# Picking and comparing neighbour marks for two graphs at once in a graph network on one core

One core of a Trainium2 chip; the metric is the time of one execution on the device in microseconds (us).

## The reference, cut to what matters

128 graphs of 64 nodes with 128 features, and a 0/1 adjacency matrix each (a seventh to an eighth of it ones). For every pair (i, j) of nodes a message is computed by a three-layer MLP, masked by the adjacency, summed over j, and the sums update the nodes by a second MLP.

```python
pair_feats = jnp.concatenate([f_i, f_j], axis=-1)
messages = _mlp(pair_feats, ...)                 # relu, layernorm, relu, layernorm, linear
messages = messages * coupling_matrix[..., None]
agg = jnp.sum(messages, axis=2)
updated = part_feats + _mlp(concatenate([part_feats, agg]), ...)
```

## The kernel before

It computes messages only where the adjacency has a one. Each graph gets 640 edge slots; two graphs make a pair (64 pairs), 512 slots a chunk (160 chunks), so five chunks serve two pairs. For a pair a 0/1 matrix `tp` says which node owns each slot. A selection on TensorE (`marks`) gives for each slot and each of 64 possible neighbours the position at which that neighbour stands; comparing with the slot's number (`compare`, VectorE) leaves a 0/1 mark at the right one. Node and neighbour marks together, 128 rows, gather the first layer's rows for each edge (`layer0`). The steps of all stages are put into a plan by chunk and place, and each engine executes its instructions in that order.

```python
        def marks(n):                                   # chunk n
            MK[n] = ps_k.tile([P, CH * P], F32, name="mk")
            for g, e, c, w in pieces(n):                # one graph at a time
                nc.tensor.matmul(MK[n][:, c:c + w], lhsT=qsall[..., g % 2, :],  # identity | positions
                                 rhs=TP[g // 2][:, e:e + w], start=True, stop=True)
        def compare(n):
            nc.vector.tensor_tensor(S[n], MK.pop(n), cmpt[:, o:o + CH * P], op=ALU.is_equal)
        def layer0(n):
            ...   # hps = abl/abh.T @ s, then h = relu(hps + b0) on ScalarE
        def root_of(q):                                 # once for five chunks
            sd = root0(stp, V0[q], QT, "m20")           # ScalarE, from GpSimd's variances
            nc.scalar.copy(SH[q][:, 0:2, :], sdb)
            nc.gpsimd.tensor_tensor(SH[q][:, 2:4, :], sdb, SH[q][:, 0:2, :]..., op=ALU.subtract)  # sh
        def turn_root(q):
            nc.tensor.transpose(SD[q][...], SH.pop(q)..., ident)                # TensorE needs sh
        ...
            # block b of four pairs starts at chunk o; all three steps run on GpSimd
            at(o - 8, "e", place, b)        # before, mid, pos
            at(o - 7, "e", place_out, b)    # pos * adjacency into the selecting weights
            at(o - 7, "e", odd_marks, b)    # two products over the adjacency
            ...
            # var0_of, root_of and turn_root of group q: chunks n and n + 1, n = 5q + 5
```

Of the kernel before, what the change touches and what calls it, by code (L numbers as in the profile page):

```python
# [9 lines left out]
F32 = mybir.dt.float32  # L10
F16 = mybir.dt.float16
F32R = mybir.dt.float32r
# [11 lines left out]
def tile_gnn(  # L24
# [9 lines left out]
    uw2: bass.AP, ub2: bass.AP,  # L34
    out: bass.AP,
):



# [65 lines left out]
    def load_first(b, q0, q1):  # L105
# [44 lines left out]
    ident = const.tile([P, P], F32, name="ident")  # L150
    make_identity(nc, ident)

    cmpt = const.tile([P, 4 * CAP], F16, name="cmpt")
    nc.gpsimd.iota(cmpt[N:P, :], pattern=[[0, 4], [1, CAP]], base=1, channel_multiplier=0,
                   allow_small_or_imprecise_dtypes=True)
    nc.vector.memset(cmpt[0:N, 0:3 * CAP // 2], 1.0)

    slot = const.tile([P, CAP], F16, name="slot")
    nc.gpsimd.iota(slot, pattern=[[2, CAP]], base=1, channel_multiplier=0,
                   allow_small_or_imprecise_dtypes=True)  # L160

    qsall = const.tile([P, 2, PB, 2, P], F16, name="qsall")
    for k in range(2):
        nc.vector.memset(qsall[:, k], 0.0)
        nc.gpsimd.tensor_copy(qsall[:, k, :, :, 0:N], ident.rearrange("p (g m) -> p g m", g=2)
                              .unsqueeze(1).to_broadcast([P, PB, 2, N]))
    ones_row = const.tile([1, P], F32, name="ones_row")

    cumall = const.tile([P, NP], F32, name="cumall")
# [120 lines left out]
    def edge_path(es):  # L290
        blkp = es.enter_context(tc.tile_pool(name="blk", bufs=3))
        adp = es.enter_context(tc.tile_pool(name="adp", bufs=2))
        tpp = es.enter_context(tc.tile_pool(name="tpp", bufs=10))
        sp = es.enter_context(tc.tile_pool(name="sp", bufs=4))
        hp = es.enter_context(tc.tile_pool(name="hp", bufs=10))
        yp = es.enter_context(tc.tile_pool(name="yp", bufs=13))
        lp = es.enter_context(tc.tile_pool(name="lp", bufs=3))
        wp = es.enter_context(tc.tile_pool(name="wp", bufs=2))
        updp = es.enter_context(tc.tile_pool(name="upd", bufs=1))
# [31 lines left out]
                fn(*args)  # L331

        blocks = {b: {} for b in range(NB)}
        TP, S, H, ST0, V0, SD, SH, Y, ST1, Q, OH, WT, YS, MK, D = ({} for _ in range(15))


        def load_adj(b):
# [7 lines left out]
        def load_x(b):  # L345
            if b < 2:
                blocks[b]["xn"] = xn0[:, b]
                return
            xn = blkp.tile([P, PB, C], F32, name="xn", bufs=7)
            nc.sync.dma_start(xn, xf[b * PB * P:(b + 1) * PB * P, :]  # L350
                              .rearrange("(q p) c -> p q c", p=P))
            blocks[b]["xn"] = xn
# [37 lines left out]
        def place_out(b):  # L390
            blk = blocks[b]
            pos = blk.pop("pos")
            for g in range(2):
                s = slice(g * N, (g + 1) * N)
                nc.gpsimd.tensor_tensor(qsall[s, b % 2, :, g, N:P], pos[s], blk["an"][s],
                                        op=ALU.mult)

        def place_first():
# [7 lines left out]
        def place_pair(q):  # L406
            blk = blocks[0]
            for g in range(2):
                s = slice(g * N, (g + 1) * N)
                nc.vector.scalar_tensor_tensor(qsall[s, 0, q, g, N:P], blk["rk"][s, q],  # L410
                                               blk["before"][s, q:q + 1], blk["an"][s, q],
                                               op0=ALU.add, op1=ALU.mult)

# [19 lines left out]
        def turn_x_out(b, q0=0, q1=PB):  # L433
            blk = blocks[b]
            if q0 == 0:
                blk["xnT"] = blkp.tile([P, PB * P], F32, name="xnT", bufs=5)
            nc.scalar.copy(blk["xnT"][:, q0 * P:q1 * P], blk.pop("x_ps")[:, q0 * P:q1 * P])

        def rows(b, half):
# [10 lines left out]

        def rows_hi(b, half):

            hi = blkp.tile([P, 4, C], F32R, name="abh", bufs=3)
            nc.scalar.copy(hi, blocks[b]["ab_ps", half].rearrange("p (k c) -> p k c", k=4))  # L454
            blocks[b]["hi", half] = hi

        def rows_lo(b, half):
            blk = blocks[b]
            hi = blk.pop(("hi", half))
            lo = blkp.tile([P, 4, C], F32R, name="abl", bufs=3)  # L460
            nc.vector.tensor_tensor(  # L461
                lo, blk.pop(("ab_ps", half)).rearrange("p (k c) -> p k c", k=4), hi.bitcast(F32),
                op=ALU.subtract)
            blk["ab", half] = (lo, hi)


        def distance(p):
            b, q = divmod(p, PB)
            D[p] = tpp.tile([P, CAP], F16, name="d", bufs=3)
            nc.scalar.activation(D[p], slot, AF.Abs, bias=blocks[b]["mid"][:, q:q + 1], scale=-1.0)  # L470

        def make_tp(p):
# [4 lines left out]
                                    op0=ALU.is_lt)  # L477
            TP[p] = tp

        def pieces(n):  # L480

            at_, end = n * CH * P, (n + 1) * CH * P
            while at_ < end:
                g, e = divmod(at_, CAP)
                w = min(end - at_, CAP - e)
                yield g, e, at_ - n * CH * P, w
                at_ += w

        def marks(n):

            MK[n] = ps_k.tile([P, CH * P], F32, name="mk")
            for g, e, c, w in pieces(n):
                nc.tensor.matmul(MK[n][:, c:c + w],  # L493
                                 lhsT=qsall[:, g // (2 * PB) % 2, g // 2 % PB, g % 2, :],
                                 rhs=TP[g // 2][:, e:e + w], start=True, stop=True)

        def compare(n):
            S[n] = sp.tile([P, CH * P], F32R, name="s")
            o = n % QC * CH * P
            nc.vector.tensor_tensor(S[n], MK.pop(n), cmpt[:, o:o + CH * P], op=ALU.is_equal)  # L500

        def layer0(n):

            ps = ps_h.tile([P, CH * P], F32, name="hps")
            s = S.pop(n)
            for g, e, c, w in pieces(n):
                for k, ab in enumerate(blocks[g // (2 * PB)]["ab", g // 4 % 2]):
                    nc.tensor.matmul(ps[:, c:c + w], lhsT=ab[:, g % 4, :], rhs=s[:, c:c + w],  # L508
                                     start=(k == 0), stop=(k == 1))
            H[n] = hp.tile([P, CH * P], F32, name="h")  # L510
            nc.scalar.activation(H[n], ps, AF.Relu, bias=b0c)  # L511
# [143 lines left out]
        def wide(name, u):  # L655

            if name not in u.blk:
                u.blk[name] = updp.tile([P, PB, C], F32, name=name,
                                        bufs=2 if name == "uo" else 1)
            return u.blk[name][:, u.q, :]  # L660

        def sums_out(u):
# [87 lines left out]
        for b in range(NB):  # L750
            o = b * CPB
            if b > 1:
                at(max(o - 25, 0), "a", load_adj, b)
                at(max(o - 20, 0), "a", load_x, b)
            if b > 0:
                r = max(o - 13, 1)
                at(max(o - 14, 0), "m", rank, b)
                at(r, "x", count, b)
                at(r + 1, "a", count_out, b)
                at(r + 1, "a", degrees, b)  # L760
                at(o - 8, "e", place, b)
                at(o - 7, "e", place_out, b)
                at(o - 7, "e", odd_marks, b)
                at(o - 4, "m", odd_weights, b)
                at(o - 3, "x", turn_x, b)
                at(o - 2, "a", turn_x_out, b)
# [34 lines left out]
                at(n + t[14], "m", finish, u)  # L801
        for p in range(NP):
            n = p * TG * 2 // CH
            if n >= 4:
                at(n - 5 if n >= 5 else 0, "a", distance, p)
                at(n - 4, "m", make_tp, p)
            w = p // 2 * QC + QC + L1 + p % 2
            last = p // 2 == NQ - 1
            at(w - 4, "a", node_marks, p)
            at(NCHK + L1 + 1 if last else w + 2, "e1", weights, p)  # L810
            at(NCHK + L1 + 2 if last else p // 2 * QC + SC, "x1", reduce, p)
# [19 lines left out]
        rank(0)  # L831
        count(0)
        count_out(0)
        nc.gpsimd.memset(cmpt[0:N, 3 * CAP // 2:4 * CAP], 1.0)
        turn_x(0, 0, 2)
        turn_x_out(0, 0, 2)
        degrees(0)
# [3 lines left out]
        make_tp(0)  # L841
        rows(0, 0)
        rows_hi(0, 0)
        distance(1)
        place_pair(1)
        make_tp(1)
        marks(0)
        rows_lo(0, 0)
        compare(0)
        nc.vector.memset(ones_row, 1.0)  # L850
        marks(1)
        compare(1)
        at(0, "x", turn_x, 0, 2, PB)
        at(0, "m", lambda: (place_pair(2), place_pair(3)))
        at(1, "a", lambda: turn_x_out_rest())
        at(1, "e", odd_marks, 0)
        at(12, "m", odd_weights, 0)
# [48 lines left out]
        for n in range(last + 1):  # L906
            run(n, "a")
            run(n, "m")
            if 0 <= n - L1 < NCHK:
                layer1(n - L1)  # L910
            run(n, "b")
            if n < NCHK:
                layer0(n)
            if 0 <= n - 1 < NCHK:
                stats0(n - 1)
            if n + 2 < NCHK:
                marks(n + 2)
                compare(n + 2)
            if 0 <= n - L1 < NCHK:
                stats1(n - L1)  # L920
            for k in ("x", "x1", "x2", "e1", "e"):
                run(n, k)
# [166 lines left out]
```

## Time and profile before

| | before |
|---|---|
| time, median of the first 3 runs | 626.22 us (625.81 to 626.4) |
| TensorE, VectorE, ScalarE, GpSimd busy | 95, 80, 56, 58% |
| a block of ten chunks in the steady stage | 35.83 us |
| granted TensorE clock, mean (1 is full speed) | 0.981 |

The profile's main lines are in the prediction below. Two lines also belong here. They are groups of the kernel before (line, engine, operation, names, shapes, count, then busy us and mean ns, then idle us before them and what ended it):

```profile
L541 PE MATMUL ma<-ident,sh 128*80 128x128 f32 x32 | 9.3, 292 | 6.8 <-POOL sh L536 5.6
L541 PEld LDWEIGHTS ma<-ident,sh 128*80 128x80 f32 x32 | 3.8, 119 | 10.5 <-POOL sh L536 10.5
```

The first line is the transpose that turns `sh`, the second the weight load (PEld) just before it; the two idle times are of one wait and are not to be added. Ten microseconds look like nothing in 625. But they say that TensorE's turn of `sh` already waits for GpSimd; in the list of waits the second line counts 18 of 32 times. A chain through a half idle engine had no slack.

### The profile page before, as it was taken

What the parts mean: (1) busy time and instruction counts of PE and PEld (TensorE: products, weight loads), DVE (VectorE), ACT (ScalarE), POOL (GpSimd) and SP (SyncE); (2) the same over time, 40 slices, a digit from 0 to 9 for tenths busy, and PEclk for the clock granted to TensorE, in tenths of its full rate; (3) what the DMA queues carried; (4) which work ended last, traced back from release to release, by engine and by line L of the source; (5) the groups of instructions that cost most, each with busy time, mean ns of one, the idle gap of its engine ahead of it and who ended that gap; (6) DMA issues with size and microseconds to landing.
All of it is one profiled execution on the core that took longest, in us unless ns stands there. A gap on an engine that the chain in (4) does not pass through costs nothing. (4 is left out here: it accounts for less than half of the span.)

```text
span 625.1 us, 15119 instructions
## 1 busy us (share of the span) xinstructions
PE 595.2 (95%) x5521; PEld 545.6 (87%) x5521; DVE 497.8 (80%) x1900; ACT 348.2 (56%) x716; POOL 363.3 (58%) x922
## 2 busy tenths in 40 slices
PE   6899999999999999999999999999999999998875
PEld 5687889999999999999999999999999999997763
DVE  7768778898878788888878789887878888885574
ACT  4565465656656565665656556665656566553412
POOL 5815264855648384664738376574838566452742
PEclk7899999999999999999999999999999999998987
DMA  4401011113030213103022211203030110201001
GB/s 120 67 2 29 12 30 39 30 34 55 1 75 12 56 32 54 33 1 86 1 60 29 56 31 28 58 3 67 21 56 22 39 24 2 60 2 40 23 18 37
DMA packets 70922, 22.52 MB, mean 36 GB/s; under 512 B 53430, under 2 KB 70844, under 8 KB 70844
## 3 DMA queue, kind: packets, MB, share of 16 engines
q1 hardware_dynamic: 70556, 21.38, 15.8%
q8 instruction: 45, 0.74, 0.5%
q14 instruction: 33, 0.27, 0.1%
q10 hardware_dynamic: 288, 0.13, 0.1%
HBM read 6.82 MB, written 4.19 MB: 18 GB/s over the span
## 5 line engine op out<-in xcount | busy, mean ns | idle before, releaser
L521 DVE BATCH_NORM_STATS2 st<-hT 128x6 f32<-128x128 f32 x640 | 140.1, 281 | 58.9 <-PE hT L517 58.5
L557 PEld LDWEIGHTS z<-w1c,h 128*128 128x128 f32 x1280 | 169.2, 192 | 7.2
L557 PE MATMUL z<-w1c,h 128*128 128x128 f32 x1280 | 169.6, 275 | 0.0
L560 ACT ACTIVATE y<-z 128x512 f32<-128x512 f32 x160 | 96.1, 601 | 107.8 <-PE z L557 107.8
L623 POOL TENSOR_TENSOR w<-oh,m_q 128x320 f32<-128x320 f16 x124 | 87.0, 723 | 115.6 <-PE mk L493 100.6
L567 DVE BATCH_NORM_STATS2 st<-y 128x6 f32<-128x128 f32 x640 | 138.0, 278 | 4.9 <-ACT y L560 4.9
L511 ACT ACTIVATE h<-hps,b0c 128x512 f32<-128x512 f32 x160 | 109.3, 683 | 5.8 <-PE hps L508 5.7
L500 DVE TENSOR_TENSOR s<-mk,cmpt 128x512 fp32r<-128x512 f32 x160 | 107.8, 674 | 0.7 <-PE mk L493 0.6
L517 PE MATMUL hT<-ident,h 128*128 128x128 f32 x640 | 97.4, 275 | 0.0
L508 PE MATMUL hps<-s,abl 128*128 128x512 f32 (+3 forms) x256 | 92.4, 373 | 0.0
L517 PEld LDWEIGHTS hT<-ident,h 128*128 128x128 f32 x640 | 76.4, 141 | 9.7
L554 PE MATMUL z<-b1t,sdT 80*128 80x512 f32 x160 | 80.5, 503 | 1.4 <-ACT y L560 1.4
L508 PE MATMUL hps<-s,abh 128*128 128x512 f32 (+3 forms) x256 | 78.8, 326 | 0.0
L638 PEld LDWEIGHTS ys<-y,w 128*64 128x64 f32 x1280 | 69.4, 137 | 9.5 <-issue 9.3
L638 PE MATMUL ys<-y,w 128*64 128x128 f32 x1280 | 77.2, 276 | 0.0
L493 PE MATMUL mk<-tp,qsall 128*128 128x512 f16 (+3 forms) x256 | 61.8, 303 | 3.5 <-DVE s L500 2.4
L461 DVE TENSOR_TENSOR abl<-mu,abh 128x512 fp32r<-128x512 f32 x32 | 22.1, 690 | 44.9 <-ACT abh L454 44.9
L470 ACT ACTIVATE d<-slot,mid 128x640 f16<-128x640 f16 x64 | 52.6, 823 | 0.7 <-DVE mid L404 0.7
L508 PEld LDWEIGHTS hps<-s,abl 128*128 128x128 f32 x256 | 49.7, 194 | 0.7 <-ACT h L511 0.4
L508 PEld LDWEIGHTS hps<-s,abh 128*128 128x128 f32 x256 | 49.8, 194 | 0.0
L454 ACT CAST abh<-mu 128x512 fp32r<-128x512 f32 x32 | 18.8, 586 | 49.3 <-PE mu L447 49.3
L554 PEld LDWEIGHTS z<-b1t,sdT 80*128 80x128 f32 x160 | 30.9, 193 | 8.1 <-issue 3.1
(219 smaller groups left out, 960.3 us busy)
## 6 DMA issues: line engine op xcount, KB each, us to landing
xn<-in_x_dram SPq DMA_DIRECT2D x15, 256.0 KB, 3.3
out_dram<-uo SPq DMA_DIRECT2D x15, 256.0 KB, 2.4
an<-in_adj_dram SPq DMA_DIRECT2D x16, 128.0 KB, 2.4
oh<-tp SPq DMA_TRANSPOSE x64, 2.5
xn<-in_x_dram SPq DMA_DIRECT2D x2, 128.0 KB
out_dram<-uo SPq DMA_DIRECT2D x2, 128.0 KB, 2.4
w<-in_L_gnn_msg_w_dram SPq DMA_DIRECT2D x2, 64.0 KB, 2.8
u<-in_L_gnn_upd_w_dram SPq DMA_DIRECT2D x2, 64.0 KB, 2.0
```

Source lines behind the costliest of these rows:

```text
L493: nc.tensor.matmul(MK[n][:, c:c + w], lhsT=qsall[:, g // (2 * PB) % 2, g // 2 % PB, g % 2, :], rhs=TP[g // 2][:, e:e + w], start=True, sto ...
L500: nc.vector.tensor_tensor(S[n], MK.pop(n), cmpt[:, o:o + CH * P], op=ALU.is_equal)
L508: nc.tensor.matmul(ps[:, c:c + w], lhsT=ab[:, g % 4, :], rhs=s[:, c:c + w], start=(k == 0), stop=(k == 1))
L511: nc.scalar.activation(H[n], ps, AF.Relu, bias=b0c)
L517: nc.tensor.transpose(ps[:, t, :], H[n][:, t * P:(t + 1) * P], ident)
L521: nc.vector.bn_stats(ST0[q][:, CH * c + t, :], ps[:, t, :])
L554: nc.tensor.matmul(ps, lhsT=SD[q], rhs=W["b1t"][:, CH * c:CH * c + CH, :], start=True, stop=False, skip_group_check=True)
L557: nc.tensor.matmul(ps[:, t, :], lhsT=h[:, t * P:(t + 1) * P], rhs=W["w1c"], start=False, stop=True, skip_group_check=True)
L560: nc.scalar.activation(Y[n], ps, AF.Relu)
L567: nc.vector.bn_stats(ST1[q][:, CH * c + t, :], Y[n][:, t, :])
L623: (nc.vector if p // 2 == NQ - 1 else nc.gpsimd).tensor_tensor(w[:, :, g, :], OH[p][:, :, g * N:(g + 1) * N], Q[q][:, k:k + TG].unsqueeze( ...
L638: nc.tensor.matmul(YS[b][g * N:(g + 1) * N, k, :], lhsT=w[:, t, g, :], rhs=y, start=(t == 0), stop=(t == TG - 1))
```

## The change

The intent: the two graphs of a pair share one selection. The weights no longer hold an identity beside one graph's positions, but the positions of both graphs; one pass over 640 columns serves both, and one comparison too. The node marks, which the identity used to bring along, are copied to f32 by ScalarE, and DMAs stack node and neighbour marks of each graph on the 128 partitions. Since this takes longer (the page of the changed kernel has 2.6 us from the issue of a neighbour stack to its landing), marks, thresholds and distances are made sooner, and with them the placing. The diff, cut to its core:

```diff
-    qsall = const.tile([P, 2, PB, 2, P], F16, name="qsall")      # identity | positions
+    posall = const.tile([P, 2, PB, 2, N], F16, name="posall")    # positions of both graphs
...
+        def node_rows(p):
+            IR[p] = tpp.tile([P, CAP], F32R, name="i32", bufs=2)
+            nc.scalar.copy(IR[p], TP[p])
+        def stack(p, half, src):
+            for g in range(2):
+                nc.sync.dma_start(S[p][half * N:(half + 1) * N, g, :]..., src[p][g * N:(g + 1) * N, :]...)
+        def marks(p, k, bank=None):                              # half k of pair p, 320 columns
+            nc.tensor.matmul(MK[p, k][:, 0:HC], lhsT=posall[...], rhs=TP[p][:, k * HC:(k + 1) * HC], ...)
+        def compare(p, k):
+            nc.vector.tensor_tensor(JR[p][:, c], MK.pop((p, k))[:, 0:HC], cmpt[:, c], op=ALU.is_equal)
...
-                at(o - 8, "e", place, b)
-                at(o - 7, "e", place_out, b)
-                at(o - 7, "e", odd_marks, b)
+                at(max(o - 11, r + 1), "e", place, b)
+                at(max(o - 10, r + 2), "e", place_out, b)
+                at(max(o - 10, r + 2), "e", odd_marks, b)
...
-                at(n - 5 if n >= 5 else 0, "a", distance, p)
-                at(n - 4, "m", make_tp, p)
+                at(max(n - 7, p - 2), "a", distance, p)
+                at(max(n - 6, p - 2), "m", make_tp, p)
+                at(max(n - 5, 1), "a", node_rows, p)
+                at(max(n - 4, 1), "a", stack, p, 0, IR)
+                for k in range(2):
+                    at(n - 5 + k, "k", marks, p, k)
+                    at(n - 5 + k, "k", compare, p, k)
+                at(n - 3, "a", stack, p, 1, JR)
```

The prologue is rewritten for the first two pairs, some pools get a buffer less to make room, and the node features of a block are loaded eight chunks later (o - 12 instead of o - 20).

More of the change, by code (lines that the diff above doesn't have):

```diff
@@ L151, in tile_gnn @@
     make_identity(nc, ident)
-    cmpt = const.tile([P, 4 * CAP], F16, name="cmpt")
-    nc.gpsimd.iota(cmpt[N:P, :], pattern=[[0, 4], [1, CAP]], base=1, channel_multiplier=0,
+    cmpt = const.tile([P, CAP], F16, name="cmpt")
+    nc.gpsimd.iota(cmpt, pattern=[[1, CAP]], base=1, channel_multiplier=0,
                    allow_small_or_imprecise_dtypes=True)
-    nc.vector.memset(cmpt[0:N, 0:3 * CAP // 2], 1.0)
     slot = const.tile([P, CAP], F16, name="slot")
@@ L160, in tile_gnn @@
                    allow_small_or_imprecise_dtypes=True)
-    qsall = const.tile([P, 2, PB, 2, P], F16, name="qsall")
-    for k in range(2):
-        nc.vector.memset(qsall[:, k], 0.0)
-        nc.gpsimd.tensor_copy(qsall[:, k, :, :, 0:N], ident.rearrange("p (g m) -> p g m", g=2)
-                              .unsqueeze(1).to_broadcast([P, PB, 2, N]))
+    posall = const.tile([P, 2, PB, 2, N], F16, name="posall")
+    nc.vector.memset(posall, 0.0)
     ones_row = const.tile([1, P], F32, name="ones_row")
@@ L292, in edge_path @@
         adp = es.enter_context(tc.tile_pool(name="adp", bufs=2))
-        tpp = es.enter_context(tc.tile_pool(name="tpp", bufs=10))
+        tpp = es.enter_context(tc.tile_pool(name="tpp", bufs=8))
         sp = es.enter_context(tc.tile_pool(name="sp", bufs=4))
-        hp = es.enter_context(tc.tile_pool(name="hp", bufs=10))
-        yp = es.enter_context(tc.tile_pool(name="yp", bufs=13))
+        hp = es.enter_context(tc.tile_pool(name="hp", bufs=9))
+        yp = es.enter_context(tc.tile_pool(name="yp", bufs=12))
         lp = es.enter_context(tc.tile_pool(name="lp", bufs=3))
@@ L333, in edge_path @@
         blocks = {b: {} for b in range(NB)}
-        TP, S, H, ST0, V0, SD, SH, Y, ST1, Q, OH, WT, YS, MK, D = ({} for _ in range(15))
+        TP, S, H, ST0, V0, SD, SH, Y, ST1, Q, OH, WT, YS, MK, D, IR, JR = ({} for _ in range(17))
         def load_adj(b):
@@ L348, in load_x @@
                 return
-            xn = blkp.tile([P, PB, C], F32, name="xn", bufs=7)
+            xn = blkp.tile([P, PB, C], F32, name="xn", bufs=6)
             nc.sync.dma_start(xn, xf[b * PB * P:(b + 1) * PB * P, :]
@@ L394, in place_out @@
                 s = slice(g * N, (g + 1) * N)
-                nc.gpsimd.tensor_tensor(qsall[s, b % 2, :, g, N:P], pos[s], blk["an"][s],
+                nc.gpsimd.tensor_tensor(posall[s, b % 2, :, g, :], pos[s], blk["an"][s],
                                         op=ALU.mult)
@@ L409, in place_pair @@
                 s = slice(g * N, (g + 1) * N)
-                nc.vector.scalar_tensor_tensor(qsall[s, 0, q, g, N:P], blk["rk"][s, q],
+                nc.vector.scalar_tensor_tensor(posall[s, 0, q, g, :], blk["rk"][s, q],
                                                blk["before"][s, q:q + 1], blk["an"][s, q],
@@ L435, in turn_x_out @@
             if q0 == 0:
-                blk["xnT"] = blkp.tile([P, PB * P], F32, name="xnT", bufs=5)
+                blk["xnT"] = blkp.tile([P, PB * P], F32, name="xnT", bufs=4)
             nc.scalar.copy(blk["xnT"][:, q0 * P:q1 * P], blk.pop("x_ps")[:, q0 * P:q1 * P])
@@ L451, in rows_hi @@
         def rows_hi(b, half):
-            hi = blkp.tile([P, 4, C], F32R, name="abh", bufs=3)
+            hi = blkp.tile([P, 4, C], F32R, name="abh", bufs=2)
             nc.scalar.copy(hi, blocks[b]["ab_ps", half].rearrange("p (k c) -> p k c", k=4))
@@ L459, in rows_lo @@
             hi = blk.pop(("hi", half))
-            lo = blkp.tile([P, 4, C], F32R, name="abl", bufs=3)
+            lo = blkp.tile([P, 4, C], F32R, name="abl", bufs=2)
             nc.vector.tensor_tensor(
@@ L468, in distance @@
             b, q = divmod(p, PB)
-            D[p] = tpp.tile([P, CAP], F16, name="d", bufs=3)
+            D[p] = tpp.tile([P, CAP], F16, name="d", bufs=2)
             nc.scalar.activation(D[p], slot, AF.Abs, bias=blocks[b]["mid"][:, q:q + 1], scale=-1.0)
@@ L478, in make_tp @@
             TP[p] = tp
+        def node_rows(p):
+            IR[p] = tpp.tile([P, CAP], F32R, name="i32", bufs=2)
+            nc.scalar.copy(IR[p], TP[p])
+        def stack(p, half, src):
+            if p not in S:
+                S[p] = sp.tile([P, 2, CAP], F32R, name="s")
+            for g in range(2):
+                nc.sync.dma_start(S[p][half * N:(half + 1) * N, g, :].bitcast(F32),
+                                  src[p][g * N:(g + 1) * N, :].bitcast(F32))
+            del src[p]
+        HC = CAP // 2
+        def marks(p, k, bank=None):
+            MK[p, k] = bank() if bank else ps_k.tile([P, 512], F32, name="mk")
+            nc.tensor.matmul(MK[p, k][:, 0:HC],
+                             lhsT=posall[:, p // PB % 2, p % PB].rearrange("p g m -> p (g m)"),
+                             rhs=TP[p][:, k * HC:(k + 1) * HC], start=True, stop=True)
+        def compare(p, k):
+            if k == 0:
+                JR[p] = tpp.tile([P, CAP], F32R, name="j32", bufs=2)
+            c = slice(k * HC, (k + 1) * HC)
+            nc.vector.tensor_tensor(JR[p][:, c], MK.pop((p, k))[:, 0:HC], cmpt[:, c],
+                                    op=ALU.is_equal)
         def pieces(n):
@@ L487, in pieces @@
                 at_ += w
-        def marks(n):
-            MK[n] = ps_k.tile([P, CH * P], F32, name="mk")
-            for g, e, c, w in pieces(n):
-                nc.tensor.matmul(MK[n][:, c:c + w],
-                                 lhsT=qsall[:, g // (2 * PB) % 2, g // 2 % PB, g % 2, :],
-                                 rhs=TP[g // 2][:, e:e + w], start=True, stop=True)
-        def compare(n):
-            S[n] = sp.tile([P, CH * P], F32R, name="s")
-            o = n % QC * CH * P
-            nc.vector.tensor_tensor(S[n], MK.pop(n), cmpt[:, o:o + CH * P], op=ALU.is_equal)
         def layer0(n):
             ps = ps_h.tile([P, CH * P], F32, name="hps")
-            s = S.pop(n)
             for g, e, c, w in pieces(n):
+                s = S[g // 2][:, g % 2, e:e + w]
                 for k, ab in enumerate(blocks[g // (2 * PB)]["ab", g // 4 % 2]):
-                    nc.tensor.matmul(ps[:, c:c + w], lhsT=ab[:, g % 4, :], rhs=s[:, c:c + w],
+                    nc.tensor.matmul(ps[:, c:c + w], lhsT=ab[:, g % 4, :], rhs=s,
                                      start=(k == 0), stop=(k == 1))
@@ L658, in wide @@
                 u.blk[name] = updp.tile([P, PB, C], F32, name=name,
-                                        bufs=2 if name == "uo" else 1)
+                                        bufs=1)
             return u.blk[name][:, u.q, :]
@@ L753, in edge_path @@
                 at(max(o - 25, 0), "a", load_adj, b)
-                at(max(o - 20, 0), "a", load_x, b)
+                at(max(o - 12, 0), "a", load_x, b)
             if b > 0:
@@ L803, in edge_path @@
             n = p * TG * 2 // CH
-            if n >= 4:
-                at(n - 5 if n >= 5 else 0, "a", distance, p)
-                at(n - 4, "m", make_tp, p)
+            if p > 1:
+                at(max(n - 7, p - 2), "a", distance, p)
[6 more added lines that the diff above has]
+                at(n - 3, "a", stack, p, 1, JR)
             w = p // 2 * QC + QC + L1 + p % 2
@@ L833, in edge_path @@
         count_out(0)
-        nc.gpsimd.memset(cmpt[0:N, 3 * CAP // 2:4 * CAP], 1.0)
         turn_x(0, 0, 2)
@@ L843, in edge_path @@
         rows_hi(0, 0)
-        distance(1)
+        S[0] = sp.tile([P, 2, CAP], F32R, name="s")
+        marks(0, 0)
+        marks(0, 1, zbank)
+        for g in range(2):
+            s = slice(g * N, (g + 1) * N)
+            nc.scalar.copy(S[0][0:N, g, :], TP[0][s])
+            for k in range(2):
+                c = slice(k * HC, (k + 1) * HC)
+                nc.vector.tensor_tensor(S[0][N:P, g, c], MK[0, k][s, 0:HC], cmpt[s, c],
+                                        op=ALU.is_equal)
+            if g == 0:
+                rows_lo(0, 0)
+                distance(1)
+        MK.pop((0, 0)), MK.pop((0, 1))
         place_pair(1)
         make_tp(1)
-        marks(0)
-        rows_lo(0, 0)
-        compare(0)
+        node_rows(1)
+        stack(1, 0, IR)
+        for k in range(2):
+            marks(1, k)
+            compare(1, k)
+        stack(1, 1, JR)
         nc.vector.memset(ones_row, 1.0)
-        marks(1)
-        compare(1)
         at(0, "x", turn_x, 0, 2, PB)
-        at(0, "m", lambda: (place_pair(2), place_pair(3)))
+        at(0, "a", lambda: place_pair(2))
+        at(1, "m", lambda: place_pair(3))
         at(1, "a", lambda: turn_x_out_rest())
@@ L915, in edge_path @@
                 stats0(n - 1)
-            if n + 2 < NCHK:
-                marks(n + 2)
-                compare(n + 2)
+            run(n, "k")
             if 0 <= n - L1 < NCHK:
```

## The prediction

> **What bounds the kernel now.** I read the page first: busy shares, slices, groups.
>
> ```profile
> PE 595.2 (95%) x5521; PEld 545.6 (87%) x5521; DVE 497.8 (80%) x1900; ACT 348.2 (56%) x716; POOL 363.3 (58%) x922
> ...
> L560 ACT ACTIVATE y<-z 128x512 f32<-128x512 f32 x160 | 96.1, 601 | 107.8 <-PE z L557 107.8
> ...
> L500 DVE TENSOR_TENSOR s<-mk,cmpt 128x512 fp32r<-128x512 f32 x160 | 107.8, 674 | 0.7 <-PE mk L493 0.6
> ...
> L493 PE MATMUL mk<-tp,qsall 128*128 128x512 f16 (+3 forms) x256 | 61.8, 303 | 3.5 <-DVE s L500 2.4
> ...
> L470 ACT ACTIVATE d<-slot,mid 128x640 f16<-128x640 f16 x64 | 52.6, 823 | 0.7 <-DVE mid L404 0.7
> ```
>
> TensorE leads, but an average over the span proves nothing, so next the busy time by stretch (columns: stretch and length, then busy us of PE, weight loads, DVE, ACT, POOL, then clock, DMA share, GB/s).
>
> ```profile
> 20.00:50.00 30.00, 26.67 (x196) 22.32 (x190) 22.21 (x81) 17.94 (x40) 13.09 (x32) 0.94 0.11 10
> 100.00:200.00 100.00, 99.71 (x967) 92.49 (x965) 82.43 (x319) 59.42 (x121) 63.29 (x161) 1.00 0.16 33
> 300.00:400.00 100.00, 99.81 (x954) 92.98 (x950) 82.24 (x318) 59.48 (x121) 60.12 (x157) 1.00 0.17 37
> ```
>
> From about 32 to 580 us TensorE has no gaps and full clock; VectorE has 17 to 18% to spare, ScalarE 40%, DMA over 80%. In this stage only work taken off TensorE's queue counts, unless something replaces it. Last the timeline of TensorE: one chunk of the steady stage, then one from the tail, where no marks are picked any more. Since matmul ends are modelled I use starts only.
>
> ```profile
> 301.58 1.06 PE L557 MATMUL z<-w1c,h 128*128 128x128 f32 x8
> 302.40 0.48 PE L508 MATMUL hps<-s,abl 128*128 128x512 f32 x1
> 302.71 0.39 PE L508 MATMUL hps<-s,abh 128*128 128x512 f32 x1
> 302.94 0.60 PE L517 MATMUL hT<-ident,h 128*128 128x128 f32 x4
> 303.38 0.38 PE L493 MATMUL mk<-tp,qsall 128*128 128x128 f16 x2
> 303.46 0.53 PE L554 MATMUL z<-b1t,sdT 80*128 80x512 f32 x1
> 303.83 1.05 PE L557 MATMUL z<-w1c,h 128*128 128x128 f32 x8
> ...
> 573.96 1.05 PE L557 MATMUL z<-w1c,h 128*128 128x128 f32 x8
> 574.77 0.48 PE L508 MATMUL hps<-s,abl 128*128 128x512 f32 x1
> 575.09 0.39 PE L508 MATMUL hps<-s,abh 128*128 128x512 f32 x1
> 575.32 0.60 PE L517 MATMUL hT<-ident,h 128*128 128x128 f32 x4
> 575.71 0.50 PE L554 MATMUL z<-b1t,sdT 80*128 80x512 f32 x1
> 576.05 1.06 PE L557 MATMUL z<-w1c,h 128*128 128x128 f32 x8
> ...
> 583.17 0.51 PE L554 MATMUL z<-b1t,sdT 80*128 80x512 f32 x1 [0.69 <-ACT y L560]
> ```
>
> From one z group to the next: 303.83 - 301.58 = 2.25 us with marks, 576.05 - 573.96 = 2.09 us without; the z matmuls take 0.81 to 0.82 us in both, so the clock is the same. A chunk's marks are thus worth 0.16 us here, not the 0.61 us of two "303 ns" instructions. The last line shows a second limit: with nothing else to do, a z (begun at 581.12 by the timeline) was followed by the next after 2.05 us, and waited for ScalarE's relu y to empty the only z bank. A chunk can't be much shorter than about 2.05 to 2.1 us.
>
> [...]302.71 to 302.94 is 230 ns for 512. [...]98 ns for a mark's f16 weights, 192 ns for z's. So mark loads hide under other matmuls, and I count columns, not instructions. [...]The trace has 2.4 to 3.3 us landings for 128 to 256 KB; it has no copy within SBUF yet.
>
> **The change, part by part.**
>
> TensorE. Before, the selecting weights hold an identity for the nodes beside the neighbour positions of one graph, so each graph's 640 slots pass separately: 64 pairs x 1280 = 81,920 columns in 256 matmuls. After, the 128 output rows are the neighbour positions of both graphs, and a pair's 640 columns pass once in two matmuls of 320: 40,960 columns, 128 matmuls. [...]Not all is to be had. Five chunks serve two pairs. Before, each had 512 mark columns; by the order of the changed program four have one matmul of 320 and the fifth none. The four save 192 columns[...]. The fifth saves the measured 0.16[...]. Against it: the chunk without marks lands on the relu limit, and the third chunk, a bare one in every other group (measured at 2.14 us), could fall to 2.06; I take off 0.05. ScalarE costs another 0.07 (below). That leaves 0.47 us. From chunk 8, where the steady stage begins, to 157 are 30 groups: 30 x 0.47 = 14.1 us; chunks 2 to 7 give perhaps 0.3.
>
> VectorE. 160 comparisons of 674 ns go; 126 of 320 columns and four half-height ones in the prologue come. [...]VectorE falls to about 452 us.
>
> ScalarE. 63 copies of the node marks to f32r, 128x640. The distance activation of that size takes 823 ns; a relu with a bias takes 683 and one without 601, so a copy is about 740 ns: 47 us more, to about 395 us (65%). In the first chunk of a group copy, distance and a square root now stand before y. From the trace, h ends its issue slot at 303.74; copy 0.62, distance 0.72, root 0.3: y starts at 305.4 instead of 304.92 and z's bank is free at about 306.05. The next z is due at 306.4 in groups whose first chunk lasts 3.17 us and 305.95 in those with 2.73: a stall of 0.1 to 0.15 in every other group, the 0.07 above.
>
> DMA. 63 x 4 = 252 copies of 64x640 f32, 164 KB each: 41 MB[...]. The issuing queue pays about 0.5 us each (0.57 for xn in the trace), about 126 us of an almost idle queue. [...]The neighbour stack is issued three chunks before its pair is gathered: for an odd pair a bare chunk 2.1, then 2.7 and 3.7, plus half a chunk, some 9 us. It is hidden.
>
> Prologue. A long index fill, a copy and memsets go; pair 0's stack is made by two ScalarE copies and four VectorE comparisons. Before, the first gather starts at 10.72 us. After, in TensorE's order, both mark matmuls of pair 1 stand ahead of it, and the second needs the bank that VectorE must compare first. Adding the prologue's durations (placing and threshold until about 6.5, comparisons and low part to 9.4, pair 1's placing and threshold to 10.4, mark, compare, mark to 11.5) I get 11.5: 0.8 late. Stack 1 lands around 16.5, where the third gather stood at 15.56. Later chunks catch up partly; I charge 0.5 us.
>
> Sum: 626.2 - 14.1 - 0.3 + 0.5 = 612.3 us.
>
> **The rivals.**
> 1. ScalarE becomes the wait. Its fillers are bunched, its order is fixed, and y and h each hold a single bank. For: the stall above. Against: 40% idle. If each group lost 0.5 us, the gain would vanish: about 625.
> 2. A stack lands late, behind a transpose or another stack, or the queue[...] is held up by a transpose waiting for its buffer. [...]Against: [...]the transposes' buffer is released four chunks ahead. A microsecond per pair would be 63 us: about 675.
> 3. VectorE, not TensorE's columns, is what paces part of the steady stage: it runs without a gap from 303.58 to 312.99 in the trace. Then shorter comparisons bring more than the columns: about 607. Against: TensorE is itself 99.8% busy.
> 4. The columns come off whole, nothing is given back[...].
>
> **Range and chances.** The steady saving should lie between 11 and 17 us, the prologue between -1 and +2. Predicted 612.3 us, range 607 to 618. The 2% mark is 613.7, just above my value: faster 0.61, same 0.35, slower 0.04 (rival 2).
>
> **What would show it.** Steps right: TensorE stays above 99% busy at mid-span; bare chunks without marks last 2.05 to 2.1 us; [...]gathers show no wait for stacks after the first three; the first gather starts at 11 to 12 us. Wrong: TensorE idle with ScalarE's y or h as releaser at the first chunk of each group (rival 1); gathers waiting for the queue (rival 2)[...].

The sum came to 626.2 - 14.1 - 0.3 + 0.5 = 612.3 us, and the 14.1 in it is 30 x 0.47. The 0.47, the 14.1, the upper end of 17 us in the range and VectorE's 452 us were estimates on rates that the profile before does not show. The profile before has 0.22 us from the first of two mark matmuls of 256 columns to what follows them (305.62 to 305.84), and in e9 a mark matmul of 320 columns and its repeat start 0.136 us apart (mean of 120). At e9's spacing 192 columns are an estimated 0.08 us and 40,960 columns 17.4 us. That mark loads hide is seen at 303.27 in the profile before: two loads, 0.21 us together, start while the hT matmuls run (from 302.94, 0.60 us).

## The result

The changed kernel takes 653.11 us (650.21 to 654.72, 4 runs) against 626.31 us (625.81 to 627.16): ratio 1.042, 95% interval 1.038 to 1.046. It is slower, and outside the predicted range. Ratios here are the mean time of one kernel's runs over that of the other's of the same rounds, so not quite the ratio of the medians.

First the page of the changed kernel, and the stretch to hold against 300 to 400 us of before.

```profile
PE 587.4 (90%) x5393; PEld 542.0 (83%) x5393; DVE 460.8 (71%) x1868; ACT 382.5 (59%) x781; POOL 356.4 (55%) x919
...
L503 DVE TENSOR_TENSOR j<-mk,cmpt 128x320 fp32r<-128x320 f32 x126 | 59.7, 473 | 1.5 <-PE mk L495 1.4
...
L479 ACT CAST i<-tp 128x640 fp32r<-128x640 f16 x63 | 45.4, 720 | 1.9 <-DVE tp L473 1.9
L554 PE MATMUL ma<-ident,sh 128*80 128x128 f32 x32 | 10.0, 312 | 38.2 <-POOL sh L549 38.1
...
s<-j SPq DMA_DIRECT2D x126, 160.0 KB, 2.6
```

```profile
300.00:400.00 100.00, 92.47 (x906) 86.38 (x903) 73.16 (x299) 61.57 (x123) 59.30 (x149) 1.00 0.46 107
```

TensorE is busy for 92.5 instead of 99.8 us in this hundred, VectorE for 73.2 instead of 82.2, GpSimd for 59.3 instead of 60.1; ScalarE alone is a little busier, 61.6 instead of 59.5. So no engine has become the bound; somebody waits. The fourth line of the page names it: the little transpose of `sh`, 32 of 15,485 instructions, has 38 us of TensorE's idle time ahead of it, ended by GpSimd. (Its weight load shows much the same idle time, of the same wait.) The new copies, on the other hand, take 720 ns (L479), where about 740 was predicted; the new comparisons take 473 ns (L503; 674 for 512 columns before).

Now the timeline around one such wait in the changed kernel: GpSimd (columns: start, length, engine, line, operation, then the idle time before it), then TensorE.

```profile
310.17 0.23 POOL L251 TENSOR_TENSOR m<-m_d,m_s 128x20 f32<-128x20 f32 x1
310.35 1.52 POOL L392 TENSOR_TENSOR posall<-pos,an 64x256 f16<-64x256 f32 x2
311.95 0.61 POOL L415 TENSOR_TENSOR a<-an 128x256 f32<-128x256 f32 x1
312.64 0.72 POOL L416 TENSOR_TENSOR a<-a,an 128x256 f32<-128x256 f32 x1
313.32 0.27 POOL L549 TENSOR_TENSOR sh<-m_sd,sh 128x40 fp32r<-128x40 f32 x1
```

```profile
309.77 1.05 PE L710 MATMUL mu<-u1c,uhT 128*128 128x128 f32 x8
313.64 0.31 PE L554 MATMUL ma<-ident,sh 128*80 128x128 f32 x1 [2.83 <-POOL sh L549]
313.71 0.47 PE L567 MATMUL z<-b1t,sdT 80*128 80x512 f32 x1
```

And the same place of a block in the kernel before:

```profile
327.83 0.23 POOL L254 TENSOR_TENSOR m<-m_d,m_s 128x20 f32<-128x20 f32 x1
328.73 0.27 POOL L536 TENSOR_TENSOR sh<-m_sd,sh 128x40 fp32r<-128x40 f32 x1 [0.68 <-ACT sh L535]
```

```profile
327.85 1.11 PE L697 MATMUL mu<-u1c,uhT 128*128 128x128 f32 x8
329.05 0.12 PEld L541 LDWEIGHTS ma<-ident,sh 128*80 128x80 f32 x1 [0.29 <-POOL sh L536]
329.06 0.31 PE L541 MATMUL ma<-ident,sh 128*80 128x128 f32 x1
```

GpSimd finishes the variances (`m`), ScalarE takes their root, GpSimd makes `sh`, TensorE turns it. Before, `sh` is done at 329.00 and taken at 329.06, and the weight load had stood idle for 0.29 us until then: nothing to spare. After, four instructions (in three lines) that nobody waits for yet, 2.9 us of them, stand in GpSimd's queue between `m` and `sh`. They are the writing of the positions and the two products of the next block, which the change moved from chunk o - 7 to chunk o - 10, where exactly this chain runs.

By chunks (starts of z, in a block of ten; the second interval shown is the one that holds the turn of `sh`):

| kernel | a chunk without marks | the chunk with `sh` | ten chunks | from the first z to the 151st |
|---|---|---|---|---|
| before | (2.22 with marks) | 3.71 | 35.83 | 535.3 |
| changed | 2.08 | 5.85 | 37.03 or 38.6 | 562.6 |

The other chunks are shorter than before, or as long in the case of one that had no marks before either: without the growth of the chunk with `sh` a block would last 34.8 us. In seven of the blocks a further 1.5 to 1.7 us goes in the next chunk or two (against the same blocks of e5 below). There the clock shows (view by stretches; the column before the last two is the granted clock): after one wait it stays at full speed, after another it drops.

```profile
384.00:390.00 6.00, 3.65 (x32) 3.40 (x30) 3.52 (x14) 2.83 (x7) 5.68 (x10) 1.00 0.52 126
...
421.00:427.00 6.00, 3.63 (x24) 3.33 (x21) 3.53 (x15) 2.00 (x5) 5.68 (x10) 0.81 0.53 128
```

The same view finds a stretch at 0.50 of the clock in all seven of these blocks, about 3.4 us long (6.8 in the first), which begins towards the end of the wait or within about a microsecond of it, and none in the other blocks up to the tail. Waits of the same 2.36 us bring it in some blocks and not in others; why is not shown.

### The profile page after: what moved, and what is told of

Read it like the earlier page. It is cut to its first block, busy times and chain, and to the rows that moved or that the text cites. A ratio compares the mean times of both kernels' runs of the same rounds, so it can differ in the third digit from the quotient of the medians.

```text
span 651.5 us, 15485 instructions
## 1 busy us (share of the span) xinstructions
PE 587.4 (90%) x5393; PEld 542.0 (83%) x5393; DVE 460.8 (71%) x1868; ACT 382.5 (59%) x781; POOL 356.4 (55%) x919
## 5 line engine op out<-in xcount | busy, mean ns | idle before, releaser
L534 DVE BATCH_NORM_STATS2 st<-hT 128x6 f32<-128x128 f32 x640 | 142.3, 285 | 106.8 <-PE hT L530 106.3
L570 PEld LDWEIGHTS z<-w1c,h 128*128 128x128 f32 x1280 | 173.9, 197 | 7.2
L570 PE MATMUL z<-w1c,h 128*128 128x128 f32 x1280 | 174.1, 280 | 0.0
L521 PE MATMUL hps<-s,abl 128*128 128x512 f32 (+3 forms) x256 | 94.6, 380 | 0.4 <-ACT h L524 0.4
L521 PE MATMUL hps<-s,abh 128*128 128x512 f32 (+3 forms) x256 | 80.5, 332 | 0.0
L503 DVE TENSOR_TENSOR j<-mk,cmpt 128x320 fp32r<-128x320 f32 x126 | 59.7, 473 | 1.5 <-PE mk L495 1.4
L521 PEld LDWEIGHTS hps<-s,abl 128*128 128x128 f32 x256 | 51.4, 201 | 1.7 <-ACT i L479 0.8
L521 PEld LDWEIGHTS hps<-s,abh 128*128 128x128 f32 x256 | 51.4, 201 | 0.0
L479 ACT CAST i<-tp 128x640 fp32r<-128x640 f16 x63 | 45.4, 720 | 1.9 <-DVE tp L473 1.9
L554 PE MATMUL ma<-ident,sh 128*80 128x128 f32 x32 | 10.0, 312 | 38.2 <-POOL sh L549 38.1
```

Of the source, the lines that this page charges most:

```text
L503: nc.vector.tensor_tensor(JR[p][:, c], MK.pop((p, k))[:, 0:HC], cmpt[:, c], op=ALU.is_equal)
L521: nc.tensor.matmul(ps[:, c:c + w], lhsT=ab[:, g % 4, :], rhs=s, start=(k == 0), stop=(k == 1))
L534: nc.vector.bn_stats(ST0[q][:, CH * c + t, :], ps[:, t, :])
L570: nc.tensor.matmul(ps[:, t, :], lhsT=h[:, t * P:(t + 1) * P], rhs=W["w1c"], start=False, stop=True, skip_group_check=True)
```

## The experiments

The theory: all of the loss is GpSimd's order, and the predicted gain is there beneath it. Rivals: ScalarE's copies delay the chain's square root (rival 1 of the prediction); the copies within SBUF slow GpSimd, the clock or the gathers (rival 2). Each kernel ran three timed rounds beside the kernel before on the same chip; all results were correct.

**e1: all three GpSimd steps back at their old chunks.**

```diff
-                at(max(o - 11, r + 1), "e", place, b)
-                at(max(o - 10, r + 2), "e", place_out, b)
-                at(max(o - 10, r + 2), "e", odd_marks, b)
+                at(o - 8, "e", place, b)
+                at(o - 7, "e", place_out, b)
+                at(o - 7, "e", odd_marks, b)
```

> The changed kernel with only its three early GpSimd steps (placing, writing the positions, squaring the marks) put back to the chunks at which the kernel before ran them. Queue theory: in the changed kernel these 2.9 us stand on GpSimd between the variances and the small subtraction sh, which TensorE waits for 2.35 us once per ten chunks; without them the wait goes, a ten-chunk block falls from 37.0 to 38.6 us to about 34.8, and the time is 612 us (610 to 616). Rival 1, ScalarE's copies delay the square root and with it GpSimd: the wait stays, 640 us or more. Rival 2, the copies within SBUF slow GpSimd or the clock: stays at 640 us or more.

Measured: 620.17 us, before 627.2, ratio 0.989 (0.986 to 0.991). Both rivals fall: the copies are all there and the wait is gone (the chunk with `sh` takes 3.59 us). But I had expected 612. The block lasts 35.44, not 34.8 us. What took the rest is in the waits (us in total, times, longest), then on ScalarE's and TensorE's timelines:

```profile
ACT d L467 <- POOL mid L381: 54.1, 13, 4.5
```

```profile
262.97 0.83 ACT L467 ACTIVATE d<-slot,mid 128x640 f16<-128x640 f16 x1 [4.38 <-POOL mid L381]
263.71 0.58 ACT L573 ACTIVATE y<-z 128x512 f32<-128x512 f32 x1
```

```profile
264.34 0.49 PE L567 MATMUL z<-b1t,sdT 80*128 80x512 f32 x1 [0.46 <-ACT y L573]
```

The change asks for the distance two chunks sooner, and the distance needs `mid`, which the placing makes. Put back, the placing is too late: ScalarE stands still for 4.4 us, its relu y comes late, and TensorE waits. So there was a reason to move the placing; there was none to move the other two with it.

**e2: the kernel before, with only these three steps moved early.**

```diff
-                at(o - 8, "e", place, b)
-                at(o - 7, "e", place_out, b)
-                at(o - 7, "e", odd_marks, b)
+                at(max(o - 11, r + 1), "e", place, b)
+                at(max(o - 10, r + 2), "e", place_out, b)
+                at(max(o - 10, r + 2), "e", odd_marks, b)
```

> The kernel before with only those three GpSimd steps moved early, as the change moves them; no stacking, no new copies. Queue theory: sh comes 2.9 us later once per ten chunks, TensorE waits some 2.3 us in about 14 blocks and sometimes loses clock after it: 655 to 668 us. Both rivals: there is neither a copy nor new traffic, so 626 us as before.

Measured: 666.65 us, ratio 1.063 (1.060 to 1.065), as expected; blocks of 38.07 us, some of 39.7. TensorE's wait is the one of the changed kernel:

```profile
396.01 0.31 PE L541 MATMUL ma<-ident,sh 128*80 128x128 f32 x1 [2.34 <-POOL sh L536]
```

There is no stacking, no copy and no new matmul in this kernel. The reordering alone costs about 39 us: some 2.2 us in each of 14 blocks, and some 1.6 us more in the five of them in which the clock drops.

**e3: the two steps one chunk later, behind `sh`; the placing stays early.**

```diff
-                at(max(o - 10, r + 2), "e", place_out, b)
-                at(max(o - 10, r + 2), "e", odd_marks, b)
+                at(max(o - 9, r + 2), "e", place_out, b)
+                at(max(o - 9, r + 2), "e", odd_marks, b)
```

> The changed kernel with the writing of positions and the squaring moved by one chunk only, so that on GpSimd they stand behind sh instead of ahead of it; placing stays early. Queue theory: it is the order on GpSimd that counts, not how early the chunk is, so the wait goes and the time is that of e1, 611 to 617 us. If being early costs by itself: stays at 640 us or more.

Measured: 629.79 us, ratio 1.004 (1.002 to 1.007): a miss. The chunk with `sh` is cured (3.58 us), as the theory has it, but another chunk of the block grew from 2.09 to 3.52 us. GpSimd carries a second chain there, the variances of the node update, and the 2.9 us now stand ahead of that one: ScalarE waits, y is late, z waits. ScalarE first, then TensorE:

```profile
268.71 0.30 ACT L271 ACTIVATE um_sq<-um_v,eps_c 128x4 f32<-128x4 f32 x1 [4.72 <-POOL um_v L265]
```

```profile
270.52 0.50 PE L567 MATMUL z<-b1t,sdT 80*128 80x512 f32 x1 [1.23 <-ACT y L573]
```

So it is the order that counts, and being behind `sh` is not enough: one has to find the place that no chain crosses.

**e4: half the dose; only the two products go back.**

```diff
-                at(max(o - 10, r + 2), "e", odd_marks, b)
+                at(o - 7, "e", odd_marks, b)
```

> The changed kernel with only the squaring (0.61 + 0.72 us) put back and the writing of positions (1.5 us) left ahead of sh. Queue theory: the wait shrinks from 2.35 to about 1.0 us per ten chunks, with fewer losses of clock: 612 + 14 x 1.0, about 627 us (623 to 633). Rivals: 640 us or more.

Measured: 627.13 us, ratio 0.999 (0.995 to 1.002), as expected. The waits for `sh` shrink from 2.35 to 0.98 us, that is by 1.37, for 1.33 us of instructions taken out of the queue; the block lasts 35.66 us. After these shorter waits the clock held: from 102 to 550 us it is granted in full.

**e5: the placing early, the other two at their old chunks.** Relative to the changed kernel:

```diff
-                at(max(o - 10, r + 2), "e", place_out, b)
-                at(max(o - 10, r + 2), "e", odd_marks, b)
+                at(o - 7, "e", place_out, b)
+                at(o - 7, "e", odd_marks, b)
```

> The changed kernel with only the placing left early (1.0 us on GpSimd, at a chunk where it is idle) and the writing of positions and the squaring at their old chunks. Queue theory: in e1 ScalarE's distance waited up to 4.4 us for the placing, because the change also asks for the distance two chunks sooner; that cost 0.53 + 0.14 us per ten chunks. Here no engine waits for GpSimd in the steady stage, a block of ten chunks takes 34.8 us instead of before's 35.8 and the time is 612 us (610 to 615), the value predicted for the change itself. If something else than GpSimd's order is in it: as e1, 620 us.

Measured: 611.51 us (611.45 to 611.79), before 626.4, ratio 0.976 (0.973 to 0.980). A block lasts 34.79 us, from the first z to the 151st are 519.7 us, and TensorE is full again at mid-span:

```profile
300.00:400.00 100.00, 99.66 (x971) 93.48 (x970) 80.75 (x326) 65.95 (x135) 63.16 (x168) 1.00 0.47 115
```

Two lines of the plan turn 4% slower into 2.4% faster. This version beats both kernels; that it does so by 2% is just not settled by its own interval, which ends at 0.9802, but e10 and e11 below, with the same two lines, are faster by that mark. The smaller pools and the later load of the features are in e5 too, so they are not what made the change slow.

**e6: e5 with another order in the prologue.** Pair 1's marks go behind the first gather, pair 2's first mark to chunk 1.

```diff
-        for k in range(2):
-            marks(1, k)
-            compare(1, k)
-        stack(1, 1, JR)
+        first_k = [(f, (1, k)) for k in range(2) for f in (marks, compare)]
+        plan[0, "k"] = first_k + [(stack, (1, 1, JR))]
...
-                    at(n - 5 + k, "k", marks, p, k)
-                    at(n - 5 + k, "k", compare, p, k)
+                    at(max(n - 5 + k, 1), "k", marks, p, k)
+                    at(max(n - 5 + k, 1), "k", compare, p, k)
```

> e5 with pair 1's mark matmuls behind the first gather on TensorE and pair 2's first mark one chunk later. Prologue theory: the first gather starts at 9.5 to 10.5 us instead of 12 to 13.5, the first z one to two us sooner, 610 to 611 us. If the prologue is paced by something else (GpSimd's first variances, the clock): as e5.

Measured: 614.26 us, ratio 0.981 (0.977 to 0.985): a miss, slower than e5. The first gather does start sooner, at 9.40 us instead of 12.04, but the first z later, at 35.9 instead of 32.9. The trace shows two things that go with it. One is VectorE's order: pair 1's first comparison now stands behind pair 2's and the next block's preparations (13.13 us; in e5 11.47), its stack follows, and the gather that needs it starts at 18.88 instead of 18.07. The other is the clock: TensorE ran at 0.50 of it from 11.2 to 21.4 and again from 31.6 to 35.0 us, in e5 only from 11.4 to 18.2. The 6.8 us more at half speed could make up the whole 3 us; how much is order and how much clock is not separated.

**e8: e5 with ScalarE's copy done twice.**

```diff
             nc.scalar.copy(IR[p], TP[p])
+            if p > 3:
+                nc.scalar.copy(IR[p], TP[p])
```

> e5 with ScalarE's copy of the node marks done twice for each pair from the fifth on: 60 x 0.72 = 43 us more on ScalarE. Rival 1 of the prediction in a milder form: ScalarE has 35% idle but its order leaves 0.07 us before the relu y in the first chunk of every other group, so a second copy costs about 0.75 us per ten chunks: e5 + 10, about 622 us. If idle share were what counts: as e5. If the copies were what made the change slow: e5 + 25 or more.

Measured: 630.42 us, ratio 1.006 (1.003 to 1.010): e5 plus 19, where I had expected 10. The block grows by 1.27 us to 36.06, and from the first z to the 151st that makes 18.3 us, nearly the whole 19. (The first z comes 1.9 us later too, but most of that is not the second copy: the first gather, which precedes any such copy, is already 1.5 us late. TensorE ran at half the pace before it: pairs of the products `mu<-w0a,xnT` and `mu<-w0b,xnT` around 7 us follow each other after 0.21 us, in e5 after 0.11, although the clock column prints 1.00 there.) In the block, the first chunk of one group grows by 0.73 us and that of the other by 0.29, because y comes late; the next chunk grows by 0.18, because the square root is late as well and with it `sh`. ScalarE, then TensorE:

```profile
256.18 0.73 ACT L481 CAST i<-tp 128x640 fp32r<-128x640 f16 x1
256.81 0.83 ACT L467 ACTIVATE d<-slot,mid 128x640 f16<-128x640 f16 x1
257.54 0.30 ACT L271 ACTIVATE m_sq<-m_v,eps_c 128x20 f32<-128x20 f32 x1
257.74 0.57 ACT L575 ACTIVATE y<-z 128x512 f32<-128x512 f32 x1
```

```profile
258.37 0.50 PE L569 MATMUL z<-b1t,sdT 80*128 80x512 f32 x1 [0.50 <-ACT y L575]
```

A third of ScalarE's time is idle, and yet it has room for one copy here and not for two.

**e9: e5 with each mark matmul done twice.**

```diff
+            if p > 3:
+                nc.tensor.matmul(MK[p, k][:, 0:HC], lhsT=..., rhs=..., start=True, stop=True)   # again
```

> e5 with each mark matmul done twice for each pair from the fifth on, into the same bank: the columns of the kernel before, with the new matmuls. Column theory: [...]e5 + 14 to 17, about 627 us, as the kernel before. If marks hide beside other matmuls: as e5.

(The 14 to 17 was an estimate.) Measured: 623.62 us, ratio 0.996 (0.992 to 1.001), e5 plus 12 rather than 14 to 17. The chunks with marks grow by 0.13 to 0.14 us each, the distance from the start of a mark matmul of 320 columns to that of its repeat (0.13 or 0.14 us, 0.136 in the mean of 120), except the one with `sh`: it shrinks from 3.59 to 3.43 us while its forerunner grows from 2.63 to 2.77, so that the two together take 6.20 instead of 6.22. That is how one sees that TensorE still waits a quarter of a microsecond for `sh` in e5; in the trace the weight load of the turn stands idle for 0.31 us there, and for 0.02 in e9. In the chunks where TensorE waits for nobody, the added columns cost their whole 0.13 to 0.14 us.

**e10: e5 with the odd pairs' distance a chunk sooner**, out of the way of the square root that begins the chain.

```diff
-                at(max(n - 7, p - 2), "a", distance, p)
+                at(max(n - 7 - p % 2, p - 2), "a", distance, p)
```

> e5 with the distance of every odd pair one chunk sooner, so that it no longer stands on ScalarE between the copy and the square root in the first chunk of each group. In e5 the chunk pair in which TensorE uses sh did not grow when marks were doubled (6.22 us, and 6.20 with double marks), so it still waits about 0.25 us for GpSimd there, and the chain to GpSimd begins with that square root. Theory: 34.79 falls to 34.5 us per ten chunks, 607 to 609 us. If the chain is not what is left: as e5, 611.5; if the distance now delays the relu in the chunk before (2.09 us, bare): slower than e5 by up to 5 us.

Measured: 611.44 us, ratio 0.975 (0.971 to 0.979), no different from e5: a miss in the sum. The block does fall, but by 0.12 us to 34.67 instead of by 0.3, and the first z came at 34.7 instead of 32.9, which takes back what the blocks bring. The late z goes with the clock: in the profiled run it stood at 0.50 from 31.5 to 38.2 us, where e5 had it in full. Whether the edit brought that about is not shown. So the gain in the block is small, and the time of the whole kernel cannot show it.

**e11: e5 with 240 more copies within SBUF.**

```diff
+            if p > 3:
+                for g in range(2):
+                    nc.sync.dma_start(spare[half * N:(half + 1) * N, g, :],
+                                      src[p][g * N:(g + 1) * N, 0:256].bitcast(F32))
```

> e5 with 240 more copies within SBUF, 64 KB each, issued right behind the stacks from the same buffers into a tile that nobody reads: twice the number of stacking copies and 40% more of their bytes. If stacking is hidden with several us to spare: as e5, 611 to 614 us, and no gather waits. Rival 2[...]: gathers wait, 630 us or more.

Measured: 610.03 us, ratio 0.974 (0.970 to 0.978), as e5; blocks of 34.78 us. The share of the DMA queue's transfers rose from 44.9% (in e10, which has e5's transfers) to 55.8%, and TensorE's list of waits names no transfer. Stacking is hidden with room to spare; rival 2 is out.

Blocks of ten chunks side by side, in us: before 35.83, e2 38.07; changed 37.03, e4 35.66, e3 36.20, e1 35.44, e5 34.79, e10 34.67, e11 34.78, e9 35.58, e8 36.06. (Of before, changed and e2 this is the usual block; some are longer by the loss of clock or the rarer longer waits.)

## Why the prediction was wrong

- **The step that failed is the sum, "626.2 - 14.1 - 0.3 + 0.5 = 612.3": it has no term for GpSimd.** The working goes through TensorE, VectorE, ScalarE, DMA and the prologue; the three moved lines of the plan were in the diff, and I did not cost them, since they add no instruction. The runs put the term at about +40 us: the changed kernel is 653.1 - 611.5 = 41.6 us above e5, which differs from it by two of these lines alone, and the same reordering, the placing included, costs the kernel before 666.65 - 627.2 = 39 us (e2). The size follows from the traces: against e5 the chunk with `sh` is longer by 2.2 to 2.7 us in 14 blocks, 32 us; seven blocks lose 1.5 to 1.7 us more at half clock, 11 us; and e5 loses some 1.6 us in its tail, at half clock from 554.3 to 557.5 us, that the changed kernel does not. "Slower" had been given a chance of 0.04, and for another reason (rival 2).
- **The evidence was in the profile before.** The weight load of `sh` waited for GpSimd in 18 of 32 cases, and the chain of short steps across GpSimd, ScalarE and TensorE ended with nothing to spare. The prediction looked for slack in busy shares ("ScalarE 40%") and used no reading of GpSimd at all; its busy share is printed there and not discussed. Its list of rivals allowed for a wait behind ScalarE and behind a transfer, not behind GpSimd.
- **TensorE's columns: right.** Predicted 0.47 us per five chunks; e5 gives (35.83 - 34.79)/2 = 0.52. From the first z to the 151st e5 saves 15.6 us where 14.1 + 0.3 was predicted. The bare chunk without marks was to last 2.05 to 2.1 us: 2.08. It was 2.22 with 512 columns of marks, so it saves 0.14 us (0.16 predicted), and that is less than its columns, which at e9's 0.136 us for 320 would be an estimated 0.22; why is not shown. The 0.07 us taken off for ScalarE did not come: in e5 TensorE waits for y three times in all, 1.6 us. With the plan mended the chip gives 611.5 where 612.3 was predicted. That it is so near is partly luck: the steady saving is 1.2 us larger than said, and stretches at half clock worth some 1.6 us come and go from one profiled run to the next. One reading was loose: before, the clock was not full "from about 32 to 580 us" but stood at 0.50 from 567.5 to 570.7.
- **VectorE: right.** 461 us in all (452 predicted), with 473 ns a comparison.
- **ScalarE: size right, and near the edge.** 720 ns a copy (740); its busy time rose to 382 us and not to 395. The distance, of the same size, takes 823 ns before and 834 in the changed kernel. Rival 1 did not happen in the change itself, but e8 shows how near it is: one more such copy takes back all the gain.
- **DMA: right.** Stacks of 160 KB land in 2.6 to 2.7 us (the estimate of it is cut), with about half a microsecond of issue on the queue each (medians 0.51 and 0.55 us in the changed kernel); the issue had been put at about 0.5. With the 240 further copies of e11 the time stays at 610.03 us, which shows the room.
- **Prologue: too small, and open in part.** First gather at 12.17 us (11.5), first z 1.0 us later than before (0.5). Kernels with the same prologue had their first z between 32.8 and 34.9 us, so this part is not known better than to 2 us. The clock goes with the spread: in e1, e3, e4 and e8, where the products around 7 us came at half the pace (see e8), the first gather started at 13.5 us, in the others at 11.9 to 12.3; e10 had half clock from 31.5 us. e6, meant to mend it, made it worse.
- **The stated signs worked.** "TensorE stays above 99% busy at mid-span" failed at first sight (92.5%), and the releaser named in its idle time led to the cause in one look.

## What to carry to other kernels

A step that is moved and not changed can have a cost: it goes ahead of something in its engine's queue (39 us in e2, where nothing else was changed). Before moving one, find the chains of short steps that cross that engine and end at the bound engine, and look how much time lies between the last of them and its use; a busy share says nothing about that (GpSimd was 58% busy before the change, and 2.9 us put ahead of its chain became waits of about 2.35 us a block). And when a change makes one thing needed sooner, move that thing alone: here the placing had to go, and the two steps that went along with it cost 40 us.
